# Four graph layers on one core: layer 3's scores for three of four blocks, the fourth transposed, and another order of steps

## The chip, the cores and the metric

The kernel runs on one core of one Trainium2 chip. The number that counts is the device time of one execution in microseconds (us), the median of several runs. Times of single instructions come from a profile of one execution, taken by the hardware profiler; they are in us unless marked ns. Engines: PE is TensorE's matmul, PEld its weight load, DVE is VectorE, ACT is ScalarE, POOL is GpSimd, and SP issues the transfers.

## The reference

64 graphs of 256 nodes with 256 features each pass through four layers. Each layer adds its result to its input and normalizes.

```python
x = _layernorm(x + L0(x, adj, ...))   # 4-head attention with projections, masked by adj
x = _layernorm(x + L1(x, adj, ...))   # 8-head attention of the normalized x with itself, then a feed-forward block
x = _layernorm(x + L2(x, adj, W, a))  # GAT: scores are sums of two vectors
x = _layernorm(x + L3(x, adj, a0, a1, a2, a3))

def _L3_gnn_ref(hidden, adj, a0, a1, a2, a3):
    def edge_score(a):
        s = jnp.einsum('bid,bjd->bij', hidden * a, hidden)
        return jax.nn.leaky_relu(s, LEAKY_SLOPE)
    ...
    alpha = jnp.where(adj == 1, e0, NEG_INF)      # and e1, e2, e3 for adj == 2, 3, 4
    ...
    alpha = jax.nn.softmax(alpha, axis=-1)
    return jnp.matmul(alpha, hidden)
```

In layer 3, `s[i, j]` is the sum over d of `hidden[i, d] * a[d] * hidden[j, d]`, so `s[i, j] = s[j, i]`. The adjacency of `setup_inputs` holds only 0 and 1 and is symmetric too, so of the four score matrices only the one with `a0` is used, and mask and scores are the same both ways. (The kernel checks what it assumes of the input as it goes, and has a second, general program behind it for other inputs, which does not run here.)

## The kernel before

Two graphs (a pair, `G = 2`) are worked on at a time; there are 32 pairs. A pair is a Python generator, which records its instructions in steps; several pairs are in work at once, in an order of steps that a string gives. Every matmul and transpose is tied to the one before it, so TensorE's order is the program's.

Layer 3 and the products that it shares with layer 2 (`QB = 2` blocks of `P = 128` nodes, `N = 256`, `NC = 2` halves of the features):

```python
def values_of(e, v, one, x, rs, gs, var=None):
    y = act.tile([P, TB, D], F32, name="y")
    for t in blocks_of(gs):                         # 4 blocks of queries: 2 graphs x 2
        i, q = divmod(t, QB)
        po = ps_m.tile([P, one + 1], F32, name="pm")
        for kc in range(QB):
            matmul(po, e[:, i, kc, q * P:(q + 1) * P], v[:, i * QB + kc, 0:one + 1],
                   start=kc == 0, stop=kc == QB - 1)
        r = rs[:, t:t + 1]
        nc.vector.reciprocal(r, po[:, one:one + 1])
        nc.vector.scalar_tensor_tensor(y[:, t, :], po[:, 0:D], r, x[:, t, 0:D], ALU.mult, ALU.add)
    yield
    return (yield from renormed(y, gs, var))

def layer3(g, x, mask, gs):
    ...                                             # xT: x transposed; xa: the same times a0
    yield
    ps = ps_s.tile([P, G, QB, N], F32, name="ps")
    for i in gs:
        for kc in range(QB):                        # keys on partitions, 256 queries along the free axis
            for c in range(NC):
                matmul(ps[:, i, kc, :], xT[:, c, i * N + kc * P:i * N + (kc + 1) * P],
                       xa[:, c, i * N:(i + 1) * N], start=c == 0, stop=c == NC - 1)
    ...
    nc.scalar.activation(eg, ps, AF.Exp, bias=shift)                  # line 854
    nc.scalar.activation(low, ps, AF.Exp, bias=shift, scale=SLOPE)    # line 855
    nc.vector.tensor_tensor(eg, eg, low, ALU.max)                     # line 856
    nc.vector.tensor_tensor(eg, eg, mask..., ALU.mult)                # line 857
    yield
    return (yield from values_of(e, x, D, x, r_3[:, g], gs, last[:, g]))
```

The accumulators `pm` come from a pool of four PSUM buffers, which all layers share, and the scores `ps` from one of two.

Layer 1's attention: in a step its scores (`ps<-xT`, line 516 like every matmul), ScalarE's exp (line 593), VectorE's mask (line 601), and the products of the scores of the step before (`pm<-e,z`):

```python
es = scores(i, cs, qT, kT, mask[:, i, :], hd, scale, sums)
if before:
    products(*before)
...
# in scores(), for layer 1: two exps, and eight masks with a sum each
nc.scalar.activation(e, ps, AF.Exp, scale=scale)                                   # line 593
nc.vector.scalar_tensor_tensor(e[:, h, k], e[:, h, k], 1.0, mask[:, k], ALU.mult, ALU.mult,
                               accum_out=sums[:, kc, c, j:j + 1])                   # line 601
# in products() of layer 0: the sums are tallied on ScalarE
nc.vector.reciprocal(sums, pz)                                                      # line 629
nc.scalar.activation(pz, sums, AF.Copy, accum_out=tally[i])                         # line 630
```

Other lines that are spoken of: GpSimd's `x + beta` of layer 0 (line 705), the normalization's scaling (line 547), the product of layer 0's output with 1/sum (`oT`, line 718) ahead of its output projection, and the feed-forward block (`pm<-xT,L_gnn_W` with 512 columns, `pm<-L_gnn_W,hT` with 256).

The order of steps: each digit is an age, that is how many periods ago a pair was begun; at each digit the pair of that age does its next step.

```python
ORDER = "14202302132441323211321321210212012010021010"
...
next(groups[0])
for period in range(len(groups) + int(max(ORDER))):
    if period + 1 < len(groups):
        next(groups[period + 1])          # the next pair's loads
    for age in ORDER:
        g = period - int(age)
        if 0 <= g < len(groups):
            next(groups[g], END)
```

Of the kernel before, what the change touches and what calls it, by code (L numbers as in the profile page):

```python
# [8 lines left out]
F32 = mybir.dt.float32  # L9
# [3 lines left out]
AF = mybir.ActivationFunctionType  # L13
ALU = mybir.AluOpType
AX = mybir.AxisListType

P = 128
N = 256
D = 256
NC = D // P  # L20
G = 2
QB = N // P
TB = G * QB
# [5 lines left out]
SLOPE = 0.2  # L29
# [4 lines left out]
AT_ONCE = 3  # L34


ORDER = "14202302132441323211321321210212012010021010"
PREPARE = 5


# [355 lines left out]
def usual_input(ctx: ExitStack, tc: tile.TileContext, a: dict, out: bass.AP, flag: bass.AP):  # L396
# [7 lines left out]
    nc = tc.nc  # L404
# [4 lines left out]
    act = ctx.enter_context(tc.tile_pool(name="act", bufs=AT_ONCE))  # L409
    att = ctx.enter_context(tc.tile_pool(name="att", bufs=2))  # L410
    small = ctx.enter_context(tc.tile_pool(name="small", bufs=8))
    ps_s = ctx.enter_context(tc.tile_pool(name="ps_s", bufs=2, space=bass.MemoryType.PSUM))
    ps_m = ctx.enter_context(tc.tile_pool(name="ps_m", bufs=4, space=bass.MemoryType.PSUM))
# [3 lines left out]
    ident = const.tile([P, P], F32, name="ident")  # L417
# [3 lines left out]
    shift = const.tile([P, 1], F32, name="shift")  # L421
# [12 lines left out]
    r_3 = const.tile([P, B // G, TB], F32, name="r_3")  # L434
    last = const.tile([P, B // G, TB], F32, name="last")
# [71 lines left out]
    def in_order(ins):  # L507

        if on_pe:
            tc.add_manual_dep(ins.ins, on_pe.pop(),  # L510
                              mybir.DependencyInfo(mybir.DependencyClass.NoSync, mybir.DependencyReason.DATA),
                              reason="the order of the program")
        on_pe.append(ins.ins.name)

    def matmul(*args, **kw):
        in_order(nc.tensor.matmul(*args, **kw))  # L516

    def transpose(*args):
        in_order(nc.tensor.transpose(*args))  # L519
# [32 lines left out]
    def blocks_of(gs):  # L552
        return range(gs[0] * QB, (gs[-1] + 1) * QB)

    def tokens(gs):
        return slice(gs[0] * N, (gs[-1] + 1) * N)

    def to_psum(src, c, gs=ALL):

        pt = ps_m.tile([P, T], F32, name="pm")  # L560
        for t in blocks_of(gs):
            transpose(pt[:, t * P:(t + 1) * P], src[:, t, c * P:(c + 1) * P], ident)
        return pt

    def transposed(src, scale=None, bias=None, gs=ALL):

        on = tokens(gs)
        dst = act.tile([P, NC, T], F32, name="xT")
        for c in range(NC):
            pt = to_psum(src, c, gs)  # L570
            if scale is None:
                nc.scalar.copy(dst[:, c, on], pt[:, on])
            else:
                nc.scalar.activation(dst[:, c, on], pt[:, on], AF.Identity, bias=bias[:, c:c + 1], scale=scale[:, c:c + 1])  # L574
        return dst
# [203 lines left out]
    def renormed(y, gs, var=None):  # L779

        xn = act.tile([P, TB, W], F32, name="xn")
        nc.gpsimd.memset(xn[:, :, D:D + 1], 1.0)
        for i in gs:
            mv, rstd = stats(y, i)
            if var is not None:
                nc.gpsimd.tensor_copy(var[:, i * QB:(i + 1) * QB], mv[:, :, 1])
            scaled(xn, y, i, mv, rstd[:, 0])
        yield
        return xn

    def values_of(e, v, one, x, rs, gs, var=None):

        y = act.tile([P, TB, D], F32, name="y")
        for t in blocks_of(gs):
            i, q = divmod(t, QB)
            po = ps_m.tile([P, one + 1], F32, name="pm")
            for kc in range(QB):
                matmul(po, e[:, i, kc, q * P:(q + 1) * P], v[:, i * QB + kc, 0:one + 1],
                       start=kc == 0, stop=kc == QB - 1)
            r = rs[:, t:t + 1]  # L800
            nc.vector.reciprocal(r, po[:, one:one + 1])
# [4 lines that stand above are left out]
    def layer2(x, mask, gs):  # L806
        xT = transposed(x, gs=gs)
        yield

        wh = act.tile([P, TB, W], F32, name="v")  # L810
        nc.gpsimd.memset(wh[:, :, D + 3:D + 4], 1.0)
        for tb in blocks_of(gs):
            pm = ps_m.tile([P, D + 3], F32, name="pm")
            for c in range(NC):
                matmul(pm, xT[:, c, tb * P:(tb + 1) * P], wx[:, c, :], start=c == 0, stop=c == NC - 1)
            nc.scalar.copy(wh[:, tb, 0:D + 3], pm)
        yield


        ex = small.tile([P, TB, 3], F32, name="ex")  # L820
        at = slice(gs[0] * QB, (gs[-1] + 1) * QB)
        nc.scalar.activation(ex[:, at], wh[:, at, D:D + 3], AF.Exp)
        pt = ps_m.tile([P, G, N], F32, name="pm")
        for t in blocks_of(gs):
            transpose(pt[:, t // QB, t % QB * P:(t % QB + 1) * P], ex[:, t, 0:1].to_broadcast([P, P]), ident)
        e = act.tile([P, G, QB, N], F32, name="qT")
        for t in blocks_of(gs):
            i, kc = divmod(t, QB)
            nc.vector.tensor_scalar(e[:, i, kc, :], pt[:, i, :], ex[:, t, 1:2], ex[:, t, 2:3], ALU.mult, ALU.max)
        eg = e[:, gs[0]:gs[-1] + 1].rearrange("p g k q -> p (g k q)")  # L830
        nc.vector.tensor_tensor(eg, eg, mask[:, gs[0]:gs[-1] + 1].rearrange("p g k -> p (g k)"), ALU.mult)
        yield
        return (yield from values_of(e, wh, D + 3, x, small.tile([P, TB], F32, name="r"), gs))

    def layer3(g, x, mask, gs):
        xT = act.tile([P, NC, T], F32, name="xT")
        xa = act.tile([P, NC, T], F32, name="z")
        on = tokens(gs)
        for c in range(NC):
            pt = to_psum(x, c, gs)  # L840
            nc.scalar.copy(xT[:, c, on], pt[:, on])
            nc.scalar.activation(xa[:, c, on], pt[:, on], AF.Identity, scale=a0[:, c:c + 1])
        yield
        ps = ps_s.tile([P, G, QB, N], F32, name="ps")
        for i in gs:
            for kc in range(QB):
                for c in range(NC):
                    matmul(ps[:, i, kc, :], xT[:, c, i * N + kc * P:i * N + (kc + 1) * P],
                           xa[:, c, i * N:(i + 1) * N], start=c == 0, stop=c == NC - 1)

        e = act.tile([P, G, QB, N], F32, name="qT")
        low = act.tile([P, G, QB, N], F32, name="kT")
        eg, low, ps = [t[:, gs[0]:gs[-1] + 1].rearrange("p g k q -> p (g k q)") for t in (e, low, ps)]
        nc.scalar.activation(eg, ps, AF.Exp, bias=shift)
        nc.scalar.activation(low, ps, AF.Exp, bias=shift, scale=SLOPE)
        nc.vector.tensor_tensor(eg, eg, low, ALU.max)
        nc.vector.tensor_tensor(eg, eg, mask[:, gs[0]:gs[-1] + 1].rearrange("p g k -> p (g k)"), ALU.mult)  # L857
        yield
        return (yield from values_of(e, x, D, x, r_3[:, g], gs, last[:, g]))

    def group(g):
        x, adj = (first, second)[g] if g < 2 else load_group(g)
# [19 lines left out]
        def others(gs):  # L882

            yield from project(y, hT, w2, both, b2m, gs)
            x = yield from renormed(y, gs)
            x = yield from layer2(x, mask, gs)
            x = yield from layer3(g, x, mask, gs)
            i, j = g * G + gs[0], g * G + gs[-1] + 1
            nc.sync.dma_start(out[i:j].rearrange("b (q p) d -> p (b q) d", p=P), x[:, gs[0] * QB:(gs[-1] + 1) * QB, 0:D])
# [70 lines left out]


    groups = [group(g) for g in range(B // G)]
    next(groups[0])
    preparing = prepare()
    own = 0
    for period in range(len(groups) + int(max(ORDER))):
        if period + 1 < len(groups):
            next(groups[period + 1])
        for age in ORDER:
            g = period - int(age)  # L970
            if 0 <= g < len(groups):
                next(groups[g], END)
            if age == "0" and period == 0:
                own += 1
                if own >= PREPARE:
                    next(preparing, END)
    assert all(next(g, END) == END for g in groups)

# [14 lines left out]
    pm = ps_m.tile([P, 1], F32, name="pm")  # L993
# [38 lines left out]
```

## Time and profile before

| | |
|---|---|
| median of 3 runs | 2715.65 us (2715.27 to 2715.88) |
| the profiled execution's span | 2711.9 us |
| granted TensorE clock, mean | 0.989 |
| ScalarE, layer 3: exp of 128x1024 (lines 854, 855) | 1113 and 1106 ns |
| VectorE, layer 3: maximum and mask of 128x1024 (lines 856, 857) | 1217 and 1225 ns |
| transfers | 31 GB/s on average |

The page's second part cuts the span into 40 slices and gives each engine's busy share in tenths. The granted clock is full (9 or more tenths) in all slices but the first and the last. After a ramp of some 130 us, one period is like the next; each finishes one pair. How the busy time of an engine is divided is seen in the groups of instructions by line and shape; what an engine waited for, in the list of waits and in its timeline, which gives each stretch of like instructions with its start, its length and the idle time before it.

### The profile page before, as it was taken

Reading aid. Unit: us, or ns where it says so; the run is one execution under the profiler, and the core shown is the slowest. Engines: PE = TensorE matmul, PEld = TensorE weight load, DVE = VectorE, ACT = ScalarE, POOL = GpSimd, SP = SyncE. Lnnn points to the kernel's source line nnn. Section 1 sums busy time; section 2 is a strip of 40 time slices with the busy share of each in tenths; the row PEclk is TensorE's granted clock in tenths of the full one; section 3 lists DMA queues with packets and bytes.
Section 4 is the critical chain, followed back from the end, with each engine's and each line's share of the span. In section 5 each row is a group of like instructions: output and inputs, shape, how many; then the busy total and the mean of one; then the engine's idle time right before and its main releaser. Section 6 shows DMA issues by size and latency. Waiting matters only on the chain.

```text
span 2711.9 us, 44575 instructions
## 1 busy us (share of the span) xinstructions
PE 2643.0 (97%) x16584; PEld 1782.5 (66%) x16584; DVE 1985.5 (73%) x6156; ACT 1292.0 (48%) x1962; POOL 586.7 (22%) x1139
## 2 busy tenths in 40 slices
PE   5899999999999999999999999999999999999996
PEld 3466667666667666666666666666676666666665
DVE  4667777777777777777777777777787777777774
ACT  3445545445545445545455444455444454454442
POOL 1112222212222212222222222222222222222121
PEclk7999999999999999999999999999999999999998
DMA  5001011000010010110010110000110000000000
GB/s 152 24 9 28 28 36 29 31 28 29 28 36 27 30 32 24 32 36 25 27 36 23 34 36 25 28 29 28 36 36 24 28 28 28 28 28 16 17 9 17
DMA packets 113727, 83.18 MB, mean 31 GB/s; under 512 B 44256, under 2 KB 113120, under 8 KB 113504
## 3 DMA queue, kind: packets, MB, share of 16 engines
q1 hardware_dynamic: 112416, 79.74, 9.7%
q8 instruction: 133, 2.18, 0.3%
q14 instruction: 90, 0.74, 0.1%
q10 hardware_dynamic: 1088, 0.53, 0.1%
HBM read 54.80 MB, written 17.04 MB: 26 GB/s over the span
## 4 chain that ended last, share of the span: by engine, by line
PE 84%; DVE 11%; POOL 2%; issue 1%; DMA 1%; SPq 1%; ACT 0%; POOLq 0%; DVEq 0%; ACTq 0%
PE pm L516 67%; PE ps L516 11%; PE pm L519 6%; DVE xn L547 3%; DVE e L601 3%; POOL rstd L539 2%; DVE st L532 1%; DVE y L687 1%; SPq L873 1%; POOL ve L535 1%; DVE mv L533 0%; DMA adj<-in_adj 0%; DVE zs L629 0%; DVE y L802 0%; DVE y L730 0%
## 5 line engine op out<-in xcount | busy, mean ns | idle before, releaser
L601 DVE SCALAR_TENSOR_TENSOR e<-e,mask 128x256 f32<-128x256 f32 x1024 | 363.4, 419 | 156.3 <-ACT e L593 156.3
L516 PE MATMUL pm<-L_gnn_W,hT 128*128 128x256 f32 x2048 | 466.1, 381 | 0.0
L516 PE MATMUL pm<-xT,L_gnn_W 128*128 128x512 f32 x1024 | 459.3, 596 | 0.5
L593 ACT ACTIVATE e<-ps 128x1024 f32<-128x1024 f32 x384 | 371.8, 1020 | 140.3 <-PE ps L516 123.7
L516 PEld LDWEIGHTS pm<-L_gnn_W,hT 128*128 128x128 f32 x2048 | 384.1, 190 | 65.2 <-issue 13.1
L774 ACT ACTIVATE hT<-pm,b 128x512 f32<-128x512 f32 x256 | 176.8, 691 | 416.5 <-PE pm L516 413.2
L535 POOL TENSOR_SCALAR ve<-mv 128x2 f32<-128x2 f32 x384 | 94.9, 247 | 1133.8 <-DVE mv L533 1132.1
L547 DVE TENSOR_SCALAR xn<-y,mv,rstd 128x256 f32<-128x256 f32 x384 | 207.0, 567 | 177.6 <-POOL rstd L539 177.6
L516 PEld LDWEIGHTS pm<-xT,L_gnn_W 128*128 128x128 f32 x1024 | 189.7, 190 | 210.3 <-issue 176.7
L539 POOL TENSOR_TENSOR rstd<-ve,mhalf 128x2 f32<-128x2 f32 (+1 forms) x384 | 299.7, 780 | 26.6
L532 DVE BATCH_NORM_STATS2 st<-y 128x6 f32<-128x256 f32 x768 | 299.1, 407 | 6.7
L760 POOL TENSOR_TENSOR both<-y,xb 128x512 f32<-128x512 f32 x64 | 81.2, 1269 | 691.7 <-DVE y L759 691.7
L516 PE MATMUL pm<-e,z 128*32 128x256 f32 x2048 | 178.5, 386 | 3.8 <-DVE e L601 0.7
L595 DVE TENSOR_TENSOR e<-e,mask 128x1024 f32<-128x1024 f32 x128 | 150.8, 1220 | 16.9 <-ACT e L593 16.9
L516 PE MATMUL ps<-xT 32*128 32x256 f32 x2048 | 149.0, 402 | 0.6 <-ACT e L593 0.4
L516 PEld LDWEIGHTS ps<-xT 32*128 32x128 f32 x2048 | 93.5, 185 | 73.3 <-issue 67.9
L574 ACT ACTIVATE xT<-pm,beta,gamma 128x512 f32<-128x512 f32 x128 | 92.3, 769 | 89.6 <-PE pm L519 89.5
L699 ACT ACTIVATE qT<-pm,bq 128x512 f32<-128x512 f32 x64 | 44.0, 687 | 184.8 <-PE pm L516 184.8
L516 PE MATMUL pm<-e,v 128*32 128x256 f32 x2048 | 125.9, 386 | 5.3 <-DVE e L595 5.3
L516 PE MATMUL pm<-L_gnn_WoT,oT 128*128 128x256 f32 x512 | 118.5, 386 | 10.3 <-DVE oT L718 10.3
L516 PE MATMUL pm<-xn,qT 128*128 128x257 f32 x512 | 122.0, 392 | 6.3 <-DVE qT L857 6.3
L516 PE MATMUL ps<-qT,kT 64*128 64x256 f32 x1024 | 127.9, 389 | 0.3 <-ACT e L593 0.3
(133 smaller groups left out, 4161.0 us busy)
## 6 DMA issues: line engine op xcount, KB each, us to landing
x<-in_x SPq DMA_DIRECT2D x32, 512.0 KB
adj<-in_adj SPq DMA_DIRECT2D x32, 512.0 KB
rr<-lines SPq DMA_DIRECT2D x128, 128.0 KB
out<-xn SPq DMA_DIRECT2D x31, 512.0 KB
L_gnn_W<-in_L_gnn_W SPq DMA_DIRECT2D x2, 1024.0 KB
adjT<-adjb SPq DMA_TRANSPOSE x128
lines<-zs SPq DMA_DIRECT2D x64, 4.0 KB
out<-xn SPq DMA_DIRECT2D x2, 256.0 KB
```

The lines of the kernel that those rows point to most:

```text
L516: in_order(nc.tensor.matmul(*args, **kw))
L519: in_order(nc.tensor.transpose(*args))
L532: nc.vector.bn_stats(st[:, q, :], src[:, t, 0:D])
L535: nc.gpsimd.tensor_scalar(ve[:, 0], mv[:, :, 1], EPS, None, ALU.add)
L539: nc.gpsimd.tensor_tensor(rstd, ve, mhalf[:, 0:k * QB].rearrange("p (k t) -> p k t", k=k), ALU.pow)
L547: nc.vector.tensor_scalar(dst[:, t, 0:D], src[:, t, 0:D], mv[:, q, 0:1], rstd[:, q:q + 1], ALU.subtract, ALU.mult)
L574: nc.scalar.activation(dst[:, c, on], pt[:, on], AF.Identity, bias=bias[:, c:c + 1], scale=scale[:, c:c + 1])
L593: nc.scalar.activation(e, ps, AF.Exp, scale=scale)
L595: nc.vector.tensor_tensor(e, e, mask.unsqueeze(1).to_broadcast([P, 2, QB * N]), ALU.mult)
L601: nc.vector.scalar_tensor_tensor(e[:, h, k], e[:, h, k], 1.0, mask[:, k], ALU.mult, ALU.mult, accum_out=sums[:, kc, c, j:j + 1])
L760: nc.gpsimd.tensor_tensor(both[:, i * QB:(i + 1) * QB, 0:D], o, xi, ALU.add)
L774: nc.scalar.activation(hT[:, f, :], pm, AF.Gelu, bias=b1[:, f:f + 1])
```

## The change

Layer 3's scores are a symmetric matrix of 2 x 2 blocks per graph. The changed kernel computes both blocks of the first keys and, for the second keys, only the second queries; exp, maximum and mask run over these three blocks. The fourth block is the transpose of one of them: TensorE transposes it after the mask, into a tile of the shared pool, and ScalarE copies it to its place. `values_of`, for layers 2 and 3, takes the second queries of both graphs first, as these don't need the transposed block. The order of steps is another one; the loads are now a step of their own in it (age 0), so all ages are one higher. It is meant to take work from TensorE and to arrange the steps anew around what remains.

```diff
-ORDER = "14202302132441323211321321210212012010021010"
+ORDER = "011225334342343542234235432323132121321132121"
...
-        for t in blocks_of(gs):
+        for t in sorted(blocks_of(gs), key=lambda t: -(t % QB)):
...
-                matmul(po, e[:, i, kc, q * P:(q + 1) * P], v[:, i * QB + kc, 0:one + 1],
+                matmul(po, e(i, kc, q), v[:, i * QB + kc, 0:one + 1],
...
-        ps = ps_s.tile([P, G, QB, N], F32, name="ps")
+        ps = ps_s.tile([P, G, QB * N], F32, name="ps")
+        e = act.tile([P, G, QB * N], F32, name="qT")
+        low = act.tile([P, G, N + P], F32, name="kT")
         for i in gs:
-            for kc in range(QB):
+            for kc, q0 in enumerate((0, P)):
                 for c in range(NC):
-                    matmul(ps[:, i, kc, :], xT[:, c, i * N + kc * P:i * N + (kc + 1) * P],
-                           xa[:, c, i * N:(i + 1) * N], start=c == 0, stop=c == NC - 1)
...
+                    matmul(ps[:, i, kc * N:(kc + 1) * N - q0], xT[:, c, i * N + kc * P:i * N + (kc + 1) * P],
+                           xa[:, c, i * N + q0:(i + 1) * N], start=c == 0, stop=c == NC - 1)
+
+        g0, g1 = gs[0], gs[-1] + 1
+        most = e[:, g0:g1, 0:N + P]
+        nc.scalar.activation(most, ps[:, g0:g1, 0:N + P], AF.Exp, bias=shift)
+        nc.scalar.activation(low[:, g0:g1], ps[:, g0:g1, 0:N + P], AF.Exp, bias=shift, scale=SLOPE)
+        nc.vector.tensor_tensor(most, most, low[:, g0:g1], ALU.max)
+        for to, of in ((slice(0, N), slice(0, N)), (slice(N, N + P), slice(N + P, 2 * N))):
+            nc.vector.tensor_tensor(e[:, g0:g1, to], e[:, g0:g1, to], mask[:, g0:g1, of], ALU.mult)
+        yield
+        pt = ps_m.tile([P, G, P], F32, name="pm")
+        for i in gs:
+            transpose(pt[:, i, :], e[:, i, P:N], ident)
+        nc.scalar.copy(e[:, g0:g1, N + P:2 * N], pt[:, g0:g1, :])
+
+        at = ((0, P), (N + P, N))
+        return (yield from values_of(lambda i, kc, q: e[:, i, at[kc][q]:at[kc][q] + P], x, D, x, r_3[:, g], gs, last[:, g]))
...
     groups = [group(g) for g in range(B // G)]
-    next(groups[0])
...
     for period in range(len(groups) + int(max(ORDER))):
-        if period + 1 < len(groups):
-            next(groups[period + 1])
         for age in ORDER:
             g = period - int(age)
             if 0 <= g < len(groups):
                 next(groups[g], END)
-            if age == "0" and period == 0:
+            if g == 0:
                 own += 1
-                if own >= PREPARE:
+                if own > PREPARE:
                     next(preparing, END)
```

The last lines keep a few setup computations behind the same steps of the first pair as before.

More of the change, by code (lines that the diff above doesn't have):

```diff
@@ L832, in layer2 @@
         yield
-        return (yield from values_of(e, wh, D + 3, x, small.tile([P, TB], F32, name="r"), gs))
+        return (yield from values_of(lambda i, kc, q: e[:, i, kc, q * P:(q + 1) * P], wh, D + 3, x, small.tile([P, TB], F32, name="r"), gs))
     def layer3(g, x, mask, gs):
@@ L843, in layer3 @@
         yield
-        ps = ps_s.tile([P, G, QB, N], F32, name="ps")
+        ps = ps_s.tile([P, G, QB * N], F32, name="ps")
+        e = act.tile([P, G, QB * N], F32, name="qT")
+        low = act.tile([P, G, N + P], F32, name="kT")
         for i in gs:
-            for kc in range(QB):
+            for kc, q0 in enumerate((0, P)):
                 for c in range(NC):
-                    matmul(ps[:, i, kc, :], xT[:, c, i * N + kc * P:i * N + (kc + 1) * P],
-                           xa[:, c, i * N:(i + 1) * N], start=c == 0, stop=c == NC - 1)
[L851 to L857, printed above, removed]
-        yield
-        return (yield from values_of(e, x, D, x, r_3[:, g], gs, last[:, g]))
+                    matmul(ps[:, i, kc * N:(kc + 1) * N - q0], xT[:, c, i * N + kc * P:i * N + (kc + 1) * P],
[7 more added lines that the diff above has]
+            nc.vector.tensor_tensor(e[:, g0:g1, to], e[:, g0:g1, to], mask[:, g0:g1, of], ALU.mult)
+        yield
+        pt = ps_m.tile([P, G, P], F32, name="pm")
[4 more added lines that the diff above has]
+        return (yield from values_of(lambda i, kc, q: e[:, i, at[kc][q]:at[kc][q] + P], x, D, x, r_3[:, g], gs, last[:, g]))
     def group(g):
```

## The prediction

> **What bounds the kernel now.** I read the page's first two parts, then the chain of waits, then the list of who waited for whom, and last the timelines of single engines over one period of the steady state.
>
> The page first:
>
> ```profile
> span 2711.9 us, 44575 instructions
> PE 2643.0 (97%) x16584; PEld 1782.5 (66%) x16584; DVE 1985.5 (73%) x6156; ACT 1292.0 (48%) x1962; POOL 586.7 (22%) x1139
> PE   5899999999999999999999999999999999999996
> PE 84%; DVE 11%; POOL 2%; issue 1%; DMA 1%; SPq 1%; ACT 0%; POOLq 0%; DVEq 0%; ACTq 0%
> ```
>
> TensorE is busy in every slice but the first two and the last, and the chain that ended last runs 84% through it. So what shortens TensorE's stream in the steady state shortens the kernel, and what only relieves ScalarE or VectorE does not. But "busy" is modelled: a matmul record lasts some 380 ns while the next starts 216 ns after it, so a pause shorter than the difference vanishes in the busy time. I therefore looked at the weight loads, where a pause shows. From the timelines of matmuls and of weight loads over one period (columns: start, length, engine, line, operation, tiles, form, count, and in brackets the idle time before and its releaser):
>
> ```profile
> 1291.05 1.15 PE L516 MATMUL ps<-xT 32*128 32x256 f32 x16
> 1292.12 2.38 PE L516 MATMUL pm<-e,z 128*32 128x256 f32 x16
> 1302.59 1.07 PE L516 MATMUL pm<-e,z 128*32 128x256 f32 x16
> ...
> 1292.12 0.14 PEld L516 LDWEIGHTS pm<-e,z 128*32 128x32 f32 x4 [0.33 <-DVE e L601]
> 1292.76 0.14 PEld L516 LDWEIGHTS pm<-e,z 128*32 128x32 f32 x2 [0.49 <-DVE e L601]
> 1293.45 0.16 PEld L516 LDWEIGHTS pm<-e,z 128*32 128x32 f32 x8 [0.55 <-DVE e L601]
> 1293.79 0.22 PEld L516 LDWEIGHTS pm<-e,z 128*32 128x32 f32 x2 [0.19 <-DVE e L601]
> ```
>
> The same product of layer 1 (16 records) takes 1.07 us at 1302.59 and 2.38 us at 1292.12: there its weight loads wait four times for the mask multiplication of VectorE (line 601). So TensorE loses 2.38 - 1.07 = 1.31 us. The e,z block at this place is longer by this much in each of the 30 periods between 149 and 2520 us (in the last two by a little more). The period is 81.85 us. Why VectorE is late is in its own timeline beside GpSimd's:
>
> ```profile
> 1288.22 2.76 DVE L547 TENSOR_SCALAR xn<-y,mv,rstd 128x256 f32<-128x256 f32 x2 [1.14 <-POOL rstd L539]
> 1290.90 0.41 DVE L601 SCALAR_TENSOR_TENSOR e<-e,mask 128x256 f32<-128x256 f32 x1
> ...
> 1288.15 2.35 POOL L705 TENSOR_TENSOR x<-x,beta 128x1024 f32<-128x1024 f32 x1
> ```
>
> The pair of normalizing operations takes 2.76 us here and 0.73 us at 1301.02; GpSimd adds beta to x in just that time. The eight masks that follow start 0.345 us apart, so the last ends near 1293.7, where the fourth wait ends.
>
> The layer that the change names, from the groups by shape and the timeline:
>
> ```profile
> L516 PE MATMUL ps<-z,xT 128*128 128x256 f32 x512 | 117.2, 382 | 0.4 <-ACT z L842 0.4
> ...
> 1355.58 3.62 PE L516 MATMUL ps<-z,xT 128*128 128x256 f32 x16
> ...
> 1332.37 1.03 PE L519 MATMUL pm<-ident,xb 128*128 128x128 f32 x8
> ...
> 1327.89 0.73 PEld L516 LDWEIGHTS pm<-xn,qT 128*128 128x128 f32 x4 [0.16 <-ACT pm L630]
> ```
>
> Each matmul is two records. Layer 3's scores are 16 records of 256 columns for each pair of graphs, 216 ns apart: (3620 - 380) / 15. Transposes are 109 ns apart: (1030 - 270) / 7.
>
> [...] After a pause at 343.0 us two loads of 128 FP32 columns start 108 ns apart although each is recorded with 190, [...] and I take 109 ns for a halved record. [...]
>
> **The change, part by part.**
>
> 1. *Scores.* For the second 128 keys only the second 128 queries are computed. Of the 16 records 8 shrink from 216 to 109 ns: -0.86 us for each of the 32 pairs.
>
> 2. *Transposes.* Two per pair, +0.22 us. They stand directly ahead of the products, where a switch from 32-column tiles to the whole array costs an extra first load: at present the products' first gap is 322 instead of 217 ns; a transpose's first gap after such a switch is 165 instead of 109. So -0.10 + 0.06. Together parts 1 and 2 give -0.69 us a pair; over some 31 pairs that TensorE bounds, -21 us.
>
> 3. *The copy of the transposed block and its cover.* ScalarE's order puts this copy ahead of the second tally (line 630), so it waits only for the transposes: they end some 0.45 us after they start, the copy is a 128x256 read of PSUM (0.37 us for the same size on line 841), ready at 0.9 us. The products of the second queries come first: 8 records, 1.73 us. The copy is needed at 0.27 + 1.73 + 0.43 = 2.4 us. Hidden by 1.5 us. The added PSUM tile could bring forward the wait for the tally shown in the last row above, which frees its buffer 2.6 us after the block begins. By the allocation of the changed kernel the third product takes the copy's buffer and only the fourth the tally's, at 0.27 + 2.60 = 2.9 us: no wait.
>
> 4. *ScalarE and VectorE.* Two exps over 768 instead of 1024 elements (1.11 us each now) save about 0.5 us, the copy takes 0.4; VectorE's maximum and masks save about 0.5 of 2.4 us. Neither is on the path. Only the tail of the last two graphs, a bare chain, may gain some 0.5 us.
>
> 5. *The new order of steps.* In TensorE's stream of the changed kernel three things move. (a) Before, the first scores of layer 1 were followed by the transposes of x, half a feed-forward product and the next scores, and then by the starved products. Now both halves of the feed-forward product stand in between. From the end of the scores to the products it was 0.93 + 0.22 + 3.55 + 1.08 = 5.8 us; it becomes 0.22 + 3.45 + 0.87 + 3.55 + 1.08 = 9.2. The masks end at 1293.7, 7.5 us after those scores, so the 1.31 us go. Besides, GpSimd's addition has to wait for the transposes of x, now 3.7 us later, so it no longer meets that normalization. -1.31 us x 30 = -39 us. (b) The output projection of layer 0 goes ahead of the first feed-forward matmuls, which waited 0.1 to 0.2 us for the copy of their input: about -0.1 x 30 = -3 us. (c) Loads are issued one period ahead as before. The number of switches between tilings in a period is the same.
>
> 6. *New waits.* Margins that (a) and (b) leave, from the durations above: the second set of masks is due 6.8 us after the feed-forward product ends and done at 6.3 to 6.7; layer 0's second output block is due 10.35 us after the layer 3 block begins and done at about 10.3. I allow 0.1 us a period, +3 us.
>
> Sum: -21 - 39 - 3 + 3 = -60 us, a period of about 79.85 us, and 2715.65 - 60 = 2655.6 us.
>
> **The rivals.**
>
> *R1: only the halved scores count.* The starved product finds another late mask (the second set has almost no margin), so (a) gives back what it gains: 2715.65 - 21, some 2695 us. For it: VectorE's order now puts the second normalization right ahead of the second masks, and GpSimd's addition falls on the first masks. Against it: the 3.4 us of new slack exceed the 1.3 us missing, and the first masks may lose 2.35 us and still be in time.
>
> *R2: the short records are bound by the weight load.* If a load cost its recorded 190 ns, a halved record would save 26 instead of 107 ns, 0.21 us a pair, which the transposes use up: -39 - 3 + 3, about 2676 us. Against it: the 108 ns between two loads.
>
> *R3: the transposed block stalls the products.* A late copy, or the buffer order going the other way, would cost about 0.7 us a pair, +22 us, 2677 us. Against it: the allocation and the 1.5 us of cover.
>
> *R4: a slower kernel.* It needs R3 with a stall elsewhere of over 2 us a period. Nothing in the profile speaks for it; ScalarE and VectorE both have less to do.
>
> **Range and chances.** Everything as in the sum is 2655; R1 in part, R2 or R3 move it to 2665 to 2695; ramp and tail, in which the order is only slightly changed, are worth 3 us either way. A range of 2642 to 2682 should hold it 8 times in 10. Faster by over 2% means below 2661.3 us, only 6 us above the sum, that is 0.2 us a period: 0.67. Within 2%: 0.32. Slower by over 2%: 0.01.
>
> **What would show it.** Steps 1 and 2: layer 3's scores as 8 records 216 and 8 records 109 ns apart, the block near 2.6 instead of 3.45 us. Step 3: no pause in the last eight records of the product from xn and qT; one there for ScalarE is R3. Step 5a: all layer 1 products at about 1.07 us, and the sum of weight loads waiting for line 601, 52.4 us now, down to some 15; the two operations of line 547 short at the place shown. Step 6: waits of the output projection for line 718 or of the second products for line 601. The prediction is wrong if the period is over 80.6 us, or if ramp and tail together change by over 5 us.

## The result, and the profile after

The changed kernel takes 2673.54 us (median of 6 runs, 2671.74 to 2675.4). Its time is 0.9848 of the time before, with a 95% interval of 0.9836 to 0.9861. That is 42 us less where 60 were predicted.

From the page of the kernel after: span, the engines' busy time, the chain that ended last, and two groups of VectorE.

```profile
span 2673.3 us, 44868 instructions
PE 2589.8 (97%) x16648; PEld 1764.3 (66%) x16648; DVE 1968.5 (74%) x6189; ACT 1291.3 (48%) x1995; POOL 587.3 (22%) x1139
PE 70%; DVE 17%; POOL 9%; issue 2%; DMA 1%; SPq 1%; ACT 0%; DVEq 0%; POOLq 0%; ACTq 0%
...
L601 DVE SCALAR_TENSOR_TENSOR e<-e,mask 128x256 f32<-128x256 f32 x1024 | 430.3, 486 | 131.6 <-ACT e L593 131.6
L547 DVE TENSOR_SCALAR xn<-y,mv,rstd 128x256 f32<-128x256 f32 x384 | 141.6, 410 | 180.1 <-POOL rstd L539 180.1
```

TensorE's busy share is 97% as before, and says nothing. The chain does: it now runs only 70% through TensorE and 26% through VectorE and GpSimd, where it was 84% and 13%. So TensorE now waits at the end of longer stretches of work on those two. The last two rows matter later: the normalizations of line 547 take 410 ns on average (567 before), but the masks of line 601 take 486 (419 before).

Which stretch it is shows in the list of waits of the kernel after (who waited for whom: us in all, number of waits, longest):

```profile
PEld pm L519 <- DVE z L547: 26.9, 63, 3.4
PE pm L519 <- DVE z L547: 11.5, 31, 3.1
PEld pm L516 <- DVE e L601: 6.2, 13, 1.9
```

The wait for the masks, 52.4 us before, is down to 6.2. In its place the transposes of `z` (layer 0's normalized output, which layer 1's feed-forward block takes) wait for the normalization: 63 weight loads, two for each pair in steady work (the longest, 3.4 us, lies in the ramp and is there in the kernel before too). TensorE's timeline of the kernel after, with VectorE's last `z`, and the weight loads at the wait:

```profile
1292.16 1.07 PE L516 MATMUL pm<-e,z 128*32 128x256 f32 x16
1309.12 0.44 PE L519 MATMUL pm<-ident,qT 128*128 128x128 f32 x2
1309.40 3.63 PE L516 MATMUL pm<-xn,qT 128*128 128x257 f32 x16
1324.62 3.67 PE L516 MATMUL pm<-v,qT 128*128 128x260 f32 x16
1339.30 2.78 PE L516 MATMUL ps<-z,xT 128*128 128x256 f32 x16
1345.59 0.38 PE L519 MATMUL pm<-ident,z 128*128 128x128 f32 x2
1346.18 0.41 DVE L547 TENSOR_SCALAR z<-y,mv,rstd 128x256 f32<-128x256 f32 x1
1346.25 1.16 PE L519 MATMUL pm<-ident,z 128*128 128x128 f32 x6 [0.28 <-DVE z L547]
...
1346.25 0.14 PEld L519 LDWEIGHTS pm<-ident,z 128*128 128x128 f32 x1 [0.52 <-DVE z L547]
1346.65 0.53 PEld L519 LDWEIGHTS pm<-ident,z 128*128 128x128 f32 x5 [0.26 <-DVE z L547]
```

The `e,z` products take 1.07 us, without a pause. Layer 3's scores (`ps<-z,xT`) take 2.78 us where they took 3.62 (from their start to that of the next work 2.62 where it was 3.45), and the products behind the transposed block (`xn,qT`) run through without a gap. But the eight transposes of `z`, which took 1.04 us in one piece before, are now torn in two and last until 1347.41, 1.82 us: 0.78 us of waiting. By the single records it is 0.79 us in each of 30 periods, all but the first two.

The chain of waits of the kernel after, in the microseconds ahead of this wait (start, length, what):

```profile
1343.06 0.79 DVE xb L736 x2
1343.85 0.17 DVE mv L533 x2
...
1344.10 0.22 POOL ve L535
...
1344.38 0.20 POOL ve L537
...
1344.65 1.04 POOL rstd L539
...
1345.71 0.16 DVE rstd L541
1345.87 0.33 DVE z L547
1346.20 0.07 DVE rstd L542
1346.27 0.34 DVE z L547
...
1346.65 0.77 PE pm L519 x5
```

The chain comes from one graph's normalization: the mean and variance on VectorE (line 533), the root on GpSimd (535 to 539), the scaling on VectorE (547), the transposes. In front of the last graph's line 533 stands line 736, the copy `xb` of the graph before, which the chain does not need; line 533 comes when that copy ends, at 1343.85. Followed further back, the chain passes without a gap of more than 0.08 us through layer 0's two normalizations to layer 2's products (`v,qT`). So TensorE's stretch from those products to the transposes of `z`, some 21 us, runs against an equally long chain on VectorE and GpSimd, and layer 3's scores lie inside it.

How close the race was before is read off the timeline of the kernel before, at the same place:

```profile
1358.28 0.87 DVE L736 SCALAR_TENSOR_TENSOR xb<-z,rstd,beta1r 128x256 f32<-128x256 f32 x2
1361.94 0.41 DVE L547 TENSOR_SCALAR z<-y,mv,rstd 128x256 f32<-128x256 f32 x1
1362.70 1.04 PE L519 MATMUL pm<-ident,z 128*128 128x128 f32 x8
```

The last `z` ends at 1362.35, 0.35 us before the transposes begin. After, it ends at 1346.59 (1346.18 + 0.41), 1.00 us after they begin. The fourth transpose is the first to need it, so up to 0.21 us after the beginning nothing is lost (1.00 - 0.79). The slack before was therefore 0.35 + 0.21 = 0.56 us a period.

The period, as the mean distance of 30 successive blocks of these transposes, went from 81.77 to 80.25 us: 45.7 us gained over the 30. (From one steady period to the next it is 80.31 after 81.84; the first of the 30 is shorter.) The first of them comes at 142.9 instead of 138.0 us (ramp, +4.9), and from the last of them to the end it is 123.0 instead of 120.8 us (+2.3, with the last of the waits in it). The sum is -38.5, and the span fell by 38.6.

### The profile page after: what moved, and what is told of

Read it like the earlier page. It is cut to its first block, busy times and chain, and to the rows that moved or that the text cites. A ratio compares the mean times of both kernels' runs of the same rounds, so it can differ in the third digit from the quotient of the medians.

```text
span 2673.3 us, 44868 instructions
## 1 busy us (share of the span) xinstructions
PE 2589.8 (97%) x16648; PEld 1764.3 (66%) x16648; DVE 1968.5 (74%) x6189; ACT 1291.3 (48%) x1995; POOL 587.3 (22%) x1139
## 4 chain that ended last, share of the span: by engine, by line
PE 70%; DVE 17%; POOL 9%; issue 2%; DMA 1%; SPq 1%; ACT 0%; DVEq 0%; POOLq 0%; ACTq 0%
PE pm L516 54%; PE ps L516 10%; PE pm L519 7%; POOL rstd L539 6%; DVE st L532 3%; DVE y L802 2%; DVE y L730 2%; DVE xn L547 2%; POOL ve L535 2%; DVE z L547 2%; DVE mv L533 1%; DVE y L729 1%; DVE xb L736 1%; DVE e L601 1%; DVE r L801 1%
## 5 line engine op out<-in xcount | busy, mean ns | idle before, releaser
L601 DVE SCALAR_TENSOR_TENSOR e<-e,mask 128x256 f32<-128x256 f32 x1024 | 430.3, 486 | 131.6 <-ACT e L593 131.6
L547 DVE TENSOR_SCALAR xn<-y,mv,rstd 128x256 f32<-128x256 f32 x384 | 141.6, 410 | 180.1 <-POOL rstd L539 180.1
L516 PE MATMUL pm<-e,z 128*32 128x256 f32 x2048 | 141.3, 385 | 1.7 <-DVE e L601 1.4
L516 PE MATMUL pm<-xT,L_gnn_WqT 128*128 128x512 f32 x256 | 121.5, 618 | 3.4 <-ACT xT L572 3.4
L516 PE MATMUL pm<-v,qT 128*128 128x260 f32 x512 | 119.5, 387 | 4.7 <-DVE qT L831 4.7
```

The source lines that it names most:

```text
L547: nc.vector.tensor_scalar(dst[:, t, 0:D], src[:, t, 0:D], mv[:, q, 0:1], rstd[:, q:q + 1], ALU.subtract, ALU.mult)
```

## The experiments

Periods, waits and margins are read from each run's trace in the way just shown. The expectations name theories by letter. The main ones:

- **A**: the chain through layer 2's products, layer 0's normalizations and `z` had little slack; TensorE's stretch over it became shorter by what the scores gave up, and the saving comes back as the wait.
- **A2**, a part of it: the rule "second queries first" holds for layer 2 as well, which shares `values_of` but has no transposed block to wait for. There it makes the first graph's output complete only after three of four blocks, and so delays the chain.
- **C**, the rival: GpSimd's addition of beta now meets the masks of line 601 (486 ns, 419 before), and the delay on VectorE shows as the new wait.

### The two halves of the change apart

The kernel after with the order of steps, and the driver loop, of before:

```diff
-ORDER = "011225334342343542234235432323132121321132121"
+ORDER = "14202302132441323211321321210212012010021010"
```

> Only the halved scores, the transposed block and second queries first; the order of steps is the one before. Theory A (the stretch of TensorE's stream from layer 2's products to the transposes of z only just covered a chain of VectorE and GpSimd work, 0.2 us to spare, so 0.86 us taken out of that stretch come back as a wait): some 0.65 us of wait at the transposes of z in each period, and about 2711 us, 0 to 6 below the kernel before. Theory B (the new order of steps makes the wait at z): no wait there, the full 0.69 us a period, about 2694 us. In both the starved layer 1 product (1.31 us a period) stays.

Measured: 2719.86 us, 1.0016 of before (1.0009 to 1.0023). Expected were 0 to 6 us less than before; scores for three of four blocks alone make the kernel 4 us slower. The period is 81.89 us after 81.77. The scores save their 0.69 us, and the transposes of `z` wait 0.79 us. The wait for the masks is as it was (53.1 us, after 52.4).

The kernel before with the order and the driver loop of after:

```diff
-ORDER = "14202302132441323211321321210212012010021010"
+ORDER = "011225334342343542234235432323132121321132121"
```

> Only the new order of steps; layer 3's scores whole as before, no transposes, first queries first. Theory A: the 0.86 us of scores cover the chain again, the wait at z shrinks from 0.79 us to 0.1 or less, and the time is that of the changed kernel or a little less, 2667 to 2674 us. Theory B: the wait at z stays at about 0.79 us and the time is 2694 us. In both the layer 1 product is not starved, and the ramp loses the same 5 us as in the changed kernel, if the early output projection is what loses them.

Measured: 2671.38 us, 0.9837 (0.982 to 0.9853). The order alone gives the whole gain of the change. The period is 80.18 us, 1.59 less than before: 1.31 for the masks' wait, and 0.28 more on average over the 30. From the timeline of this run:

```profile
1345.17 0.41 DVE L547 TENSOR_SCALAR z<-y,mv,rstd 128x256 f32<-128x256 f32 x1
1345.91 1.04 PE L519 MATMUL pm<-ident,z 128*128 128x128 f32 x8
```

`z` ends 0.33 us before the transposes begin, and these run through: with the longer scores there is no wait.

### What the chain carries

In the kernel after, the copy `xb` goes into the next step, so that the next graph's mean and variance stand ahead of it in VectorE's order:

```diff
             scaled(z, y, i, mv, rstd[:, 1])
+            yield
             for q, t in enumerate(blocks(i)):
                 nc.vector.scalar_tensor_tensor(xb[:, t, :], z[:, t, :], rstd[:, 0, q:q + 1], beta1r, ALU.mult, ALU.add)
-            yield
```

> The changed kernel with one thing moved: layer 0's second normalization writes z of both graphs first and the residual copy xb (two VectorE operations of 0.44 us per graph, line 736) a step later, so that the second graph's statistics reach GpSimd earlier. TensorE's order is unchanged. Theory A: z is ready 0.8 us earlier, the wait of 0.79 us at its transposes is gone or under 0.2, 29 periods x 0.6 to 0.8 = 17 to 23 us, 2650 to 2656 us. Theory C (VectorE is late since GpSimd's addition of beta now collides with its masks): the wait stays over 0.5 us, 2665 us or more.

Measured: 2653.81 us, 0.977 (0.9754 to 0.9787). An edit that removes no work gains 20 us. The last `z` comes 0.64 us earlier in relation to layer 2's products, the wait falls from 0.79 to 0.15 us, and the period to 79.64 us.

The kernel after without GpSimd's addition of beta in layer 0. This leaves a part of the computation out (with the data here beta is zero):

```diff
-        nc.gpsimd.tensor_tensor(x, x, over_blocks(beta0), ALU.add)
```

> The changed kernel without GpSimd's addition of beta to x in layer 0 (it is left out altogether; the data's beta is zero). Theory A: the masks of line 601 fall back from 486 to about 419 ns each, but the wait at z stays between 0.5 and 0.8 us, 2668 to 2674 us. Theory C: with the collision gone the wait at z goes too, about 2650 us.

Measured: 2674.2 us, 0.9845 (0.9828 to 0.9861), the time of after. The masks' group and the waits of this run:

```profile
L601 DVE SCALAR_TENSOR_TENSOR e<-e,mask 128x256 f32<-128x256 f32 x1024 | 363.6, 419 | 132.3 <-ACT e L593 132.3
```

```profile
PEld pm L519 <- DVE z L547: 26.3, 62, 3.4
```

The masks are back at 419 ns on average, so GpSimd's addition was what slowed them. But the wait for `z` stays (26.3 us, after 26.9), and so does the period, 80.23 us. C falls: the slower masks lie where VectorE has time.

The kernel after with layer 2's blocks in their natural order (layer 2 passes no `var`, layer 3 does):

```diff
-        for t in sorted(blocks_of(gs), key=lambda t: -(t % QB)):
+        for t in (blocks_of(gs) if var is None else sorted(blocks_of(gs), key=lambda t: -(t % QB))):
```

> The changed kernel, but layer 2's products take their queries in natural order (both blocks of the first graph, then of the second); layer 3 keeps the second queries first. Theory A2 (half of the wait at z comes from this order: the first graph's normalization of layer 2 starts one product later, xn at 6.40 instead of 5.05 us after the products begin, z 0.5 us later): z of the second graph back at 21.5 us after the products begin, the wait at z down from 0.79 to 0.3 to 0.4 us, 11 to 14 us off, 2659 to 2663 us. Rival (the order of queries is of no account, the chain is set by the halved scores alone): wait unchanged, 2671 to 2675 us.

Measured: 2661.25 us, 0.9796 (0.978 to 0.9812), 12 us less than after. Counted from the start of layer 2's products, the first normalization of line 547 ends at 5.05 instead of 6.40 us and the last `z` at 21.46 instead of 21.97; the wait falls to 0.29 us. A2 holds. The wait of after is now divided: 0.83 us shorter scores against 0.56 us of slack make 0.27, about what remains here, and layer 2's order made the other 0.5.

Both edits together:

```diff
-            yield                                             # behind the loop of xb
+            yield                                             # ahead of it
...
+        for t in (blocks_of(gs) if var is None else sorted(blocks_of(gs), key=lambda t: -(t % QB))):
```

> Both: layer 2 in natural order and the residual copy a step later. Theory A with A2: z ready by 20.9 us after the products begin, no wait at its transposes at all (e3 still had 0.15 us a period), a period of 79.5 us, 2648 to 2651 us. If some other part of the chain takes over, or the natural order costs elsewhere, 2653 us or more.

Measured: 2651.27 us, 0.9758 (0.9742 to 0.9774), and 2654.88 when it ran again, below. Both are above the 2648 to 2651 us expected, but the period is as expected, 79.49 us. The timeline of this run:

```profile
1332.65 0.17 DVE L533 BATCH_NORM_AGGREGATE mv<-st 128x2 f32<-128x6 f32 x1
1332.75 0.45 DVE L737 SCALAR_TENSOR_TENSOR xb<-z,rstd,beta1r 128x256 f32<-128x256 f32 x1
1335.14 0.41 DVE L547 TENSOR_SCALAR z<-y,mv,rstd 128x256 f32<-128x256 f32 x1
1335.43 1.04 PE L519 MATMUL pm<-ident,z 128*128 128x128 f32 x8
```

The variance (line 533) is now ahead of the second `xb`. `z` ends 0.12 us after the transposes begin, within the 0.21 us found above, and they run through in 1.04 us.

Two controls. The `xb` edit in the kernel before, where by A nothing waits for `z`:

```diff
             scaled(z, y, i, mv, rstd[:, 1])
+            yield
             for q, t in enumerate(blocks(i)):
                 ...                                           # xb, as above
-            yield
```

> Control: the kernel before, with only the residual copy moved a step later, as in e3. Theory A: before, the chain ended 0.2 to 0.4 us ahead of its need, so a shorter chain gains nothing: 2713 to 2718 us, the starved layer 1 product unchanged. Rival (the later copy relieves VectorE in general and would have helped any version): 2700 us or less.

Measured: 2716.17 us, a ratio of 1.0 (0.9991 to 1.0008). The edit has no value of its own.

The `xb` edit in the second kernel of these experiments (new order, old scores):

```diff
+ORDER = "011225334342343542234235432323132121321132121"
...
+            yield                                             # ahead of the loop of xb, as above
```

> The new order of steps and the later residual copy, but layer 3's scores whole as before, without transposes, all queries in natural order: e6 less the halved scores. Theory A: the chain to z is covered here (as in e2), so the period is e6's plus the full worth of the halved scores less transposes, 0.69 us: 80.18 us, 2669 to 2673 us; the difference to e6, some 20 us, is what the halved scores are worth when nothing waits. Rival (the halved scores are worth little even then): under 10 us of difference to e6, 2661 us or less.

Measured: 2670.82 us, 0.9834 (0.9818 to 0.9849); the period is 80.18 us as without the edit. This run differs from the kernel with both edits only in layer 3 (scores, transposes, order of the blocks), so the two periods give what these are worth once the chain is short: 80.18 - 79.49 = 0.69 us, 20.7 us over 30 periods. The starts of the matmuls, averaged over 24 periods, say where it lies: the scores take 0.84 us less, the transposes 0.28 more, and the products behind them 0.12 less. Beside the run of the kernel with both edits on the same chip, below, the medians differ by 15.9 us and the profiled spans by 20.8 (2669.0 and 2648.2).

### The ramp

The first transposes of `z` in steady work come 4.9 us later in the kernel after. TensorE's timelines around 116 us, first before, then after:

```profile
114.48 1.65 PE L519 MATMUL pm<-ident,xb 128*128 128x128 f32 x6 [3.82 <-DVE xb L547]
116.14 4.60 PE L516 MATMUL pm<-xT,L_gnn_W 128*128 128x512 f32 x8
120.58 3.62 PE L516 MATMUL pm<-L_gnn_WoT,oT 128*128 128x256 f32 x16
```

```profile
116.12 3.62 PE L516 MATMUL pm<-L_gnn_WoT,oT 128*128 128x256 f32 x8
121.99 2.49 PE L516 MATMUL pm<-L_gnn_WoT,oT 128*128 128x256 f32 x8 [2.26 <-DVE mv L533]
124.28 2.66 PE L516 MATMUL pm<-xT,L_gnn_W 128*128 128x512 f32 x3
```

In both kernels TensorE stands still for 3.8 us before. Then before does the feed-forward product, which is ready, and the output projection when its input is there. After has the output projection first, by the new order: eight matmul records at about half the rate (3.62 us, as long as sixteen take before), 2.26 us of waiting, and the rest. The stretches of 5 us (first the time, then each engine's busy time, then the granted clock, the DMA share and GB/s), before and after:

```profile
115.00:120.00 5.00, 4.99 (x12) 2.51 (x12) 1.04 (x2) 3.52 (x4) 0.00 (x0) 0.70 0.17 54
120.00:125.00 5.00, 5.00 (x21) 3.72 (x20) 2.46 (x7) 0.69 (x1) 0.63 (x2) 1.00 0.00 0
```

```profile
115.00:120.00 5.00, 4.74 (x14) 3.48 (x13) 0.76 (x2) 2.84 (x3) 0.00 (x0) 0.51 0.17 54
120.00:125.00 5.00, 3.01 (x9) 2.26 (x10) 4.18 (x11) 0.00 (x0) 1.25 (x2) 0.83 0.00 0
125.00:130.00 5.00, 5.00 (x11) 2.20 (x10) 4.21 (x15) 1.38 (x2) 1.48 (x4) 0.83 0.01 3
```

Shorter stretches show how the clock goes within these. Before, it is 0.50 from 114.6 to 118.0 us and 1.00 from there on. After, it is 0.50 from 113.1 to 119.9, 1.00 to 123.3, again 0.50 to 126.7, and then 1.00. So the clock recovers just as the second pause begins (119.74), and after this pause it falls to half a second time, for 3.4 us of work. The first fall is longer than before, too, but not by the order: the control with the old order and the `xb` edit has only the one pause, and its clock is at half for 6.8 us (114.3 to 121.1).

Around the first pause (3.8 us) the trace of after shows a granted clock of one half that begins within the pause (113.1 us, the pause lasts from 110.85 to 114.67), and the eight records of the output projection at 116.12 us 427 ns apart, where they are 216 apart at full clock before. The pause of 2.26 us was followed by half the clock as well. Whether the pauses bring the falls about, and how long one must be for it, is not shown.

How long TensorE takes from the first pair's transposes of `z` to the second pair's divides all the profiles in two. It is 68.4 to 69.4 us in the five without the early projection (before, the scores with the old order, the `xb` control, and twice the exchange that follows), and 72.1 to 74.2 us in the eight with it.

The kernel with both edits, with the two steps exchanged in the one period of the ramp in question:

```diff
+RAMP = "011225334343243542234235432323132121321132121"      # "23" -> "32" at one place of ORDER
...
-        for age in ORDER:
+        for age in (RAMP if period == 3 else ORDER):
```

> e6, and in the one period in which the second pair's output projection meets the first pair's feed-forward block, those two steps change places, as they stood before; every other period is e6's. Theory D (the 5 us that the ramp lost come from this place: the early projection waits for its input, TensorE pauses once more and its clock stays at half for some 8 us longer): the first transposes of z between feed-forward halves come at about 138 to 140 instead of 143 to 144 us, and 3 to 5 us are gained over e6, 2644 to 2647 us. Rival (the ramp differs for another reason, as the arrival of weights): no gain over e6.

Measured: 2648.26 us, 0.9748 (0.9732 to 0.9764), 3 us below the same kernel without the exchange, but with overlapping intervals. The trace is clearer than the times. From the stretches of this run:

```profile
115.00:120.00 5.00, 3.29 (x8) 1.95 (x9) 1.43 (x4) 2.50 (x5) 0.93 (x2) 0.67 0.28 82
120.00:125.00 5.00, 5.00 (x18) 3.15 (x17) 1.03 (x2) 1.84 (x3) 0.00 (x0) 0.99 0.00 0
```

There is no second pause, the clock recovers as before, and the first steady transposes of `z` come at 140.2 instead of 143.7 us.

As 3 us are little, both kernels ran once more, with the same edits: first with the exchange, then without.

> e8 again, beside e6 again on the same chip, as their times overlapped. Theory D: 3 to 4 us less than e6, the trace again with the first transposes of z between feed-forward halves at about 140 us. Rival: no difference.

> e6 again: 2649 to 2653 us, the first transposes of z between feed-forward halves at about 143.6 us.

Measured: with the exchange 2648.55 us (2647.68 to 2650.34), 0.9753 (0.974 to 0.9766); without 2654.88 us (2649.94 to 2655.31), 0.9772 (0.9758 to 0.9785). The first steady transposes come at 139.0 and 142.8 us. The order of the two is the same both times, and the traces differ by 3.6 and 3.8 us; the intervals of the times still touch. The medians differ by 3.0 and 6.3 us, but the five times without the exchange fall in two groups 5 us apart (2649.94 and 2650.68, then 2654.88 to 2655.31), for which no cause is shown. So the 3.7 us of the traces are the better figure for what the exchange is worth. The kernel with it is the best of all that ran, 25 us below the changed kernel.

The tail stays open. From the last transposes of `z` to the end, two profiles of the same kernel (with the exchange) show 125.5 and 122.3 us, so the 2.3 us between before and after are no more than this spread.

## Why the prediction was right and wrong, point by point

**Steps 1 and 2, scores and transposes: right in size.** A halved record follows the one before by 111 ns and a full one by 216, and scores, transposes and the products behind them measured -0.84, +0.28 and -0.12 us a period where -0.86, +0.22 and -0.04 were predicted (the prediction put the first gap of the transposes, +0.06, with the products). The net 0.69 us a period is confirmed by the period itself (the two runs that differ in layer 3 alone). With it R2 falls: a weight load of these scores is still recorded with 191 ns on average, and does not bound a record of 111. The 108 ns between two loads in the profile of before was the right guide.

**Step 3, the copy: right.** The products of `xn` and `qT` run through 16 records in one piece. R3 falls.

**Step 4, ScalarE and VectorE not on the path: right for the operations named, wrong in its sense.** Nothing of the shorter exps, maximum and masks of layer 3 shows on the path, as predicted. But the chain of VectorE and GpSimd to `z` was 0.56 us from being the bound elsewhere, and became it.

**Step 5, the order: right, with a side that was missed.** The 1.31 us at the masks went altogether (52.4 us of waiting to 6.2), and GpSimd's addition no longer meets the two normalizations (567 to 410 ns). (b) came as counted: from before to the second kernel of the experiments, the first feed-forward matmuls shrink by 0.10 us a period. The rest of the 0.28 (0.32 in steady work) was not foreseen and lies elsewhere in TensorE's stream: the transposes of `ex` take 0.18 us less, the second feed-forward matmuls 0.10, the transposes of `x` 0.06, and the projection with `WqT` 0.10 more (means over 24 steady periods; why, is not shown). The order's price in the ramp, some 4 us, was not seen: the projection put ahead has its input ready in the steady state, but not in that period of the ramp.

**Step 6, new waits: this is the step that failed.** "I allow 0.1 us a period, +3 us" was 0.79 us a period, 24 us over the 30 periods that have it. The list of margins had the second masks and layer 0's second output block. It did not have the transposes of `z`, which stand right behind the work that the change makes shorter, and whose slack was to be read in the profile of before: `z` ended 0.35 us ahead of them, and 0.21 us more could be lost. The second part, 0.5 us by layer 2's order, could be read in the diff: `values_of` is shared.

The sum with what was measured, in us over the 30 distances between 31 blocks of the transposes; 29 of the 30 waits lie within these, the last lies in the tail:

| term | predicted | measured |
|---|---|---|
| scores and transposes | -21 | 0.69 x 30 = -20.7 |
| starved products | -39 | 1.31 x 30 = -39.3 |
| output projection earlier, and what else the order gives | -3 | 0.28 x 30 = -8.4 (what was left of the period) |
| new waits | +3 | 0.79 x 29 = +22.9 |
| ramp | 0 (ramp and tail: 3 either way) | +4.9 |
| tail | 0 | +2.3 (within its spread) |
| sum | -60 | -38.3 (the spans differ by 38.6, the medians of the times by 42.1) |

**The rivals.** The time came out between the sum and R1, but not by R1's mechanism: R1 said that only the scores would count and that the order would give back its gain. It is the other way round. The order keeps its gain, and the scores give theirs back, to a wait for which no rival had been named. That the range of 2642 to 2682 us holds the time is owed to its width, which was made for rivals that did not come, and in so far it is luck; of the chances, 0.67 had gone to a gain of over 2%, where 1.5% came. Two signs were named at the end of the prediction, either of which would show it wrong. The period is not one: 80.31 us in steady work, below 80.6 (79.85 were predicted). The other came: ramp and tail together changed by 7.2 us, over 5.

## What to carry to other kernels

Before work is cut from the engine that bounds a kernel, look for what the other engines do in the shadow of this work: take the next few waits behind the cut and read how long before its need each input was ready; where that is less than the cut, the difference is lost. Such a chain can sometimes be shortened for nothing, by moving an operation that it does not need behind the one that it does (here 20 us for one moved line). A helper that several layers share carries a new order to places where it only costs, and an order of steps made for the steady state needs a look at the ramp.

## What the runs showed of the hardware that was not expected

- In the kernel after, one mask of line 601 in each period (31 of 1024) took 2.56 to 2.58 us where the others took 0.42. It began 0.14 us after GpSimd's addition of beta (2.42 us, at 1276.36) and ended 0.29 us after it; the mean of 486 ns hides this. Without the addition the longest mask took 0.43 us. The collision named in the prediction was not removed but moved from line 547 to line 601, where it happened to cost nothing.
- A pause of TensorE of 2.26 us, in the ramp, was followed by a fall of the granted clock to 0.50, which came 1.3 us after work had resumed (121.99) and lasted 3.4 us (123.3 to 126.7). After a pause of 3.8 us alone the clock was at 0.50 for 3.4 us in four profiles and for 6.8 us in a fifth, the control with the `xb` edit.
